# A gated delta-rule layer on one core: joint 32-block merges, weights loaded singly, index loads a job ahead, and a stated order for the first steps

## The chip, the core and the metric

The kernel runs on one core of a Trainium2 chip. Time is device time in microseconds of one execution. The engines run side by side, each through its own stream of instructions in program order: TensorE (PE, with its weight loads shown as PEld), VectorE (DVE), ScalarE (ACT), GpSimd (POOL) and SyncE (SP), which here issues every DMA. They wait for each other by semaphores.

## The reference

The input is x of 4 sequences x 512 positions x 256 channels, in float32. With xn the layer-normed x, the output is `x + s * silu(f)`, where f is a feed-forward whose weights come from a 16-entry table, and s the attention-like part:

```
qkvz = xn @ W_qkvz.T                  # 16 groups: q, k, 2 v, 2 z of 128 each
q, k, v = silu(causal conv of 4 taps, per channel)
beta = sigmoid(b);  g = -exp(A_log) * softplus(a + dt_bias)
q, k = rmsnorm(q), rmsnorm(k)         # scaled
per head: gated delta rule in chunks
    T = inverse of (I + tril(beta k k^T decay, -1))
    v_new = T v_beta - T (k_beta e^g) state
    out   = (q e^g) state + tril(q k^T decay) v_new
    state = state e^g_last + k^T v_new
s = (norm_w * rmsnorm(out) * silu(z)) @ W_out.T
f = (silu(xn @ lut[gate].T) * (xn @ lut[up].T)) @ lut[down].T
```

## The kernel before

The work is cut into 64 items: 4 sequences times 16 groups, each group with one q, one k and two value heads, over all 512 positions as four chunks of 128. An item goes through some 115 steps, each a short Python function in `STEPS`. `SLOT` (L965) is a list of step names with lags: in slot n each step `name:lag` is issued for item n - lag, so that in one slot about a dozen items are worked on, each at another stage. The order in which steps are issued is the order of every engine's stream. What is not there yet in the first slots (n - lag below 0), or no longer in the last, is simply left out.

The steps that the change touches:

- `ga` (L414) loads the 512 columns of the projection weights for q, k and both v of an item as one tile `wa`; `gz` those of z, `go` the output weights. `aq ak av0 av1` (L434) project, `y*` (ACT, L440) applies the last tap, `c*` (DVE, L446) the three others, `s*` the silu.
- `kk nt at` make the masked products, `nd nl` bring the 32 x 32 diagonal blocks to a layout of one block a partition group by DMA through DRAM, `L0` to `L3` (POOL, L621 and L627) invert them by substitution, `yd iu` bring them back by DMA into `iut`.
- `tp` (DVE, L648) turns diagonal blocks into `tpl`. `W` (L657) multiplies the off-diagonal block by one inverse, `wt` (ACT) negates and copies, `U` (L670) multiplies by the other inverse, `iu2` writes the 64-block's corner into `iut`, and `t10` turns that. `WU` (`merge2`, L687) does the same from 64 to 128: there `W2` of one item and `U2` of the item before are issued in turn, block by block, as one step.
- `ks r pv vn ps st` walk the state over the four chunks, `po sqo so ro o th h pp ac` make the output and add it to `acc`.
- `X` in the list pulls one piece of the table lookups (`lookups`, L299 on; DVE), two instructions on 344 or 256 columns. 14 jobs of 16 such pieces fill the feed-forward's weights; a job begins with the load of its indices (L316).
- `Y` lets `prepare` pull one piece of `both(b + 1)`: norm and gates of the next sequence (`normed`, `gated`). After a piece with PE work it waits three steps before the next. For sequence 1 this starts at slot 3.
- The feed-forward (`feed_forward`) fills PE where a step of the list has no item left; it starts at slot `total + 4`. Its last outputs, those of sequence 3, are kept until all else is done, since they need `acc` (L890, L891).

PSUM has eight banks, handed out in turn by `Bank`; `NBUF` says how many buffers a tile has.

Of the kernel before, what the change touches and what calls it, by code (L numbers as in the profile page):

```python
# [19 lines left out]
P = 128  # L20
# [13 lines left out]
for n, tags in {2: "v0 nt vt1 nl yl nd yd", 3: "wa qe v1 iut nk", 4: "q kd at vt0", 5: "eq", 6: "zT0 zT1", 8: "k"}.items():  # L34
    NBUF.update(dict.fromkeys(tags.split(), n))
# [3 lines left out]
def gated_delta_ffn_kernel(  # L39
# [181 lines left out]
    def gated(b):  # L221
# [3 lines left out]
        def tmp(name, shape):  # L225
            return prep.tile(shape, F32, tag=name, name=f"{name}_{b}")


        u, ab = (tmp(n, [P, 2, NC, HV]) for n in ("u", "ab"))
        graw, diff = (tmp(n, [P, NC, HV]) for n in ("graw", "diff"))  # L230
# [50 lines left out]
        gT = xs_of[b].rearrange("p c d -> p (c d)")[:HV, :S]  # L281
# [17 lines left out]
    def lookups():  # L299

        jobs = []
        for name, to, src in (("g", wg_d, gate_idx), ("u", wu_d, up_idx)):
            for d in range(DC):
                for half in range(2):
                    part = slice(half * LW, (half + 1) * LW)
                    jobs.append((f"{name}{d}{half}", to[d, :, part], src[d * P : (d + 1) * P, part]))
        for f in range(FC):
            n = min(P, INTER - f * P)
            jobs.append((f"d{f}", wd_d[f, :n, :], down_idx[f * P : f * P + n, :]))
        for name, to, src in jobs:  # L310
            n, width = src.shape
            ix, t, fx, w = (
                ffw.tile([P, LW], dt, tag=tag, name=f"{tag}_{name}")[:n, :width]
                for tag, dt in (("lt1", I32), ("lt0", F32), ("fx", F32), ("lw", F32))
            )
            moved(ix, src)  # L316
            yield

            nc.vector.tensor_copy(fx, ix)
            t1 = ffw.tile([P, LW], F32, tag="lt1", name=f"lt1f_{name}")[:n, :width]  # L320
            nc.vector.tensor_scalar(t, fx, 0.0, float(LUT), ALU.is_lt, ALU.mult)
            nc.vector.tensor_add(fx, fx, t)
            nc.vector.tensor_scalar(fx, fx, 0.0, float(LUT - 1), ALU.max, ALU.min)
            for k in range(LUT):
                if k > 1:
                    nc.vector.tensor_add(w, w, (t, t1)[(k - 1) % 2])
                nc.vector.tensor_scalar(
                    (t, t1)[k % 2] if k else w, fx, float(k), lut_b[:n, k : k + 1], ALU.is_equal, ALU.mult
                )
                yield  # L330
            nc.vector.tensor_add(w, w, (t, t1)[(LUT - 1) % 2])
            moved(to, w)
# [14 lines left out]
    SHAPES.update({"wa": [P, DC, 4 * P], "wz": [P, DC, NP * P], "wo": [P, NP, D]})  # L347
# [66 lines left out]
    @step("ga")  # L414
    def _(it):
        w = w_qkvz[:, it.hq * GW : it.hq * GW + 4 * P]
        moved(it.wa, w.rearrange("(c p) o -> p c o", p=P))
# [12 lines left out]
    def channels(x, g, block):  # L430
        def project(it):
            ps = it.put("a" + x, K)
            for d in range(DC):
                nc.tensor.matmul(  # L434
                    ps, lhsT=it.wa[:, d, g * P : (g + 1) * P], rhs=it.xnT[:, d, :],
                    start=(d == 0), stop=(d == DC - 1),
                )
# [18 lines left out]

    channels("q", 0, lambda hq: hq)
    channels("k", 1, lambda hq: HQK + hq)
    for p in range(NP):
        channels(f"v{p}", 2 + p, lambda hq, p=p: 2 * HQK + NP * hq + p)  # L460
# [191 lines left out]
    @step("W")  # L652
    def _(it):
        ps = it.put("pW")[:, : G * Q].rearrange("p (g i) -> p g i", g=G)
        for g in range(G):
            for lo, hi in HALVES:
                nc.tensor.matmul(ps[hi, g, :], lhsT=it.nt[lo, g, hi], rhs=it.tpl[lo, g, :Q], start=True, stop=True)  # L657
# [6 lines left out]

    @step("U")
    def _(it):
        ps = it.put("pU")[:, : G * Q].rearrange("p (g i) -> p g i", g=G)
        for g in range(G):
            for lo, hi in HALVES:
                nc.tensor.matmul(ps[lo, g, :], lhsT=it.wt[hi, g, :], rhs=it.iut[hi, g, hi], start=True, stop=True)  # L670
# [14 lines left out]


    def merge2(it, before):  # L687
        if before:
            pu = before.put("pU2").rearrange("p (g i) -> p g i", g=G)
        if it:  # L690
            pw = it.put("pW2").rearrange("p (g i) -> p g i", g=G)
        for g in range(G):
            if it:
                nc.tensor.matmul(pw[HI, g, :], lhsT=it.nt[LO, g, HI], rhs=it.tpl[LO, g, :], start=True, stop=True)  # L694
            if before:
                nc.tensor.matmul(
                    pu[LO, g, :], lhsT=before.w64[HI, g, :], rhs=before.iut[HI, g, HI], start=True, stop=True
                )

    @step("W2")  # L700
    def _(it):
        merge2(it, None)
# [4 lines left out]

    @step("U2")
    def _(it):
        merge2(None, it)  # L710
# [142 lines left out]
    def feed_forward():  # L853

        wgu = buffers("wa wz")[:FC]
# [19 lines left out]
        hs = buffers("ds nl")  # L875
        wd, fin, kept = [], [], []
# [6 lines left out]
        def two(ap):  # L883
            return ap.rearrange("p (j d) -> p j d", j=2)

        def finish(b, c2, y, s):
            at_ = slice(b * NC + 2 * c2, b * NC + 2 * c2 + 2)
            xr = two(in_turn("f", fin))
            moved(xr, x_t[:, at_, :])
            nc.vector.tensor_mul(y, y, s)  # L890
            nc.vector.tensor_add(y, y, xr)  # L891
            moved(out_t[:, at_, :], y)


        for b in (B - 2, B - 1, *range(B - 2)):
# [30 lines left out]
            if not wd:  # L926
                ws = buffers("v0 v1 q")
# [4 lines left out]
                held, fin = ws[3:5], ws[5:]  # L932
            for c2 in range(NC // 2):
                yield 4 * FC
                behind()
                bank = Bank(f"pd_{b}_{c2}", 1)
                for j in range(2):
                    c = 2 * c2 + j
                    for f in range(FC):
                        n = min(P, INTER - f * P)  # L940
                        nc.tensor.matmul(  # L941
                            two(bank.ap)[:, j, :], lhsT=hT[f][:n, c * P : (c + 1) * P], rhs=wd[f][:n],
                            start=(f == 0), stop=(f == FC - 1),
                        )

                def output(b=b, c2=c2, bank=bank):
                    last = b == B - 1
                    y = two(held[c2] if last else in_turn("f", fin))
                    silu(y, two(bank.read()))
                    if last:  # L950
                        kept.append((b, c2, y, acc[:, 2 * c2 : 2 * c2 + 2, :]))
                    else:
                        s = two(in_turn("f", fin))
                        moved(s, acc_d[2 * b + c2])
                        finish(b, c2, y, s)
# [3 lines left out]
        yield 1 << 30  # L959
        for late in kept:  # L960
            finish(*late)
# [4 lines left out]
        "so1:9 am:8 Y vn1:8 tk:4 cv02:3 cv11:3 ac1:11 ro1:9 cv12:3 iu:6 X o1:9 po0:8 yq:2 ps1:8 st1:8 "  # L966
        "ga:0 sqk:4 cq0:2 L0:5 pp0:11 z1:5 X sz0:5 sz1:5 tp:6 ks2:8 r2:8 go:10 po1:8 lk:4 W:6 ds:4 pv2:8 "
        "wt:6 ls:4 kk0:4 vn2:8 L1:5 ac0:11 U:6 cq1:2 eq:7 ps2:8 cq2:2 x0:4 ak:0 iu2:6 st2:8 sqo0:8 t10:6 "
        "kd:4 gz:4 ks3:8 WU:6 po2:8 x1:4 Y r3:8 pv3:8 vt1:6 kk1:4 iu4:7 vn3:8 X L2:5 yk:0 X pv0:7 po3:8 "
        "so0:8 nt0:4 nt1:4 tv0:4 vn0:7 w2:6 e:5 ro0:8 ps0:7 ck0:0 av0:2 sq:2 vt0:4 th1:9 yl:4 at0:4 tq:4 "  # L970
        "st0:7 av1:2 ck1:0 at1:4 th0:9 ck2:0 yv0:2 sqq:4 h1:9 ks1:7 cv00:2 o0:8 r1:7 cv01:2 h0:9 nd:4 "
        "nl:4 L3:5 yd:5 sk:2 sv1:4 tv1:5 pp1:10 pv1:7 aq:1 yv1:2 sqo1:8 cv10:2 g:3 z0:4 qm:5 sv0:3"
    )
    plan = [(name, int(lag or 0)) for name, _, lag in (key.partition(":") for key in SLOT.split())]
    last_lag = max(lag + (name == "WU") for name, lag in plan)
# [11 lines left out]
    items = []  # L987
# [15 lines left out]
    due = soon = 0  # L1003

    def prepare():

        nonlocal due, soon
        if soon:
            soon -= 1
            if soon:  # L1010
                return
        elif due and len(free) > 1:
            due -= 1
        else:
            return
        soon = 3 if next(preparing, None) else 0

    for n in range(total + last_lag):
        if n < total:
            items.append(Item(n))  # L1020
            b, hq = divmod(n, HQK)
            if hq == 3 and b + 1 < B:
                assert next(preparing, None) is None
                preparing = both(b + 1)
        if n == total + 4:
            for _ in looked:
                pass
            needed = next(feeding)
        for name, lag in plan:
            if name == "X":  # L1030
                next(looked, None)
            elif name == "Y":
                due += 1
            elif name == "WU":
                if item(n - lag) or item(n - lag - 1):
                    merge2(item(n - lag), item(n - lag - 1))
            elif item(n - lag):
                STEPS[name](item(n - lag))
                due += n < 2
                prepare()  # L1040
            elif needed is not None:
                spare += PASSES.get(name, 0)
                feed()
    for _ in feeding:
# [50 lines left out]
```

## Time and profile before

| what | us |
|---|---|
| median of three runs | 2115.0 (2111.66 to 2115.02) |
| the profiled execution, its own time | 2115.5 |
| its span, first to last instruction | 2113.8 |
| PE busy over the span | 2021.6 |
| DVE, ACT, POOL busy | 1771.2, 1627.2, 1370.1 |
| mean granted TensorE clock | 0.979 |

The busy time of an engine counts the stretches in which at least one of its instructions runs. A matmul of float32 is two passes in the trace (x2), each with its weight load. PE's ends are modelled, so consecutive passes overlap in the list: what a pass costs is the distance between starts. A slot is seen in the trace as the distance between the key projections of consecutive items.

### The profile page before, as it was taken

What the parts mean: (1) busy time and instruction counts of PE and PEld (TensorE: products, weight loads), DVE (VectorE), ACT (ScalarE), POOL (GpSimd) and SP (SyncE); (2) the same over time, 40 slices, a digit from 0 to 9 for tenths busy, and PEclk for the clock granted to TensorE, in tenths of its full rate; (3) what the DMA queues carried; (4) which work ended last, traced back from release to release, by engine and by line L of the source; (5) the groups of instructions that cost most, each with busy time, mean ns of one, the idle gap of its engine ahead of it and who ended that gap; (6) DMA issues with size and microseconds to landing.
All of it is one profiled execution on the core that took longest, in us unless ns stands there. A gap on an engine that the chain in (4) does not pass through costs nothing.

```text
span 2113.8 us, 48084 instructions
## 1 busy us (share of the span) xinstructions
PE 2021.6 (96%) x15744; PEld 1479.7 (70%) x15744; DVE 1771.2 (84%) x4338; ACT 1627.2 (77%) x4693; POOL 1370.1 (65%) x4181
## 2 busy tenths in 40 slices
PE   5689999999999999999999999999999999989997
PEld 3356777777776777777777777777777777776664
DVE  7878999999998999999999899999999888753322
ACT  2668888888887888888888888888888888874421
POOL 0477777777776777777767777777777777773000
PEclk8979999999999999999999999999999999998999
DMA  2333344334443434443334434344333343331202
GB/s 90 93 99 94 105 117 111 98 98 109 108 111 86 109 102 117 108 109 99 104 101 112 107 97 105 101 116 111 100 97 104 105 107 101 91 95 26 64 30 70
DMA packets 318538, 206.35 MB, mean 98 GB/s; under 512 B 221120, under 2 KB 283216, under 8 KB 318288
## 3 DMA queue, kind: packets, MB, share of 16 engines
q1 hardware_dynamic: 318288, 203.28, 36.1%
q8 instruction: 125, 2.05, 0.4%
q14 instruction: 125, 1.02, 0.2%
HBM read 179.05 MB, written 24.13 MB: 96 GB/s over the span
## 4 chain that ended last, share of the span: by engine, by line
PE 83%; DVE 6%; POOL 3%; DMA 3%; ACT 1%; issue 1%; SPq 1%; POOLq 0%; DVEq 0%; ACTq 0%
PE pp L823 10%; PE av L434 9%; PE pz L466 9%; PE pv L745 5%; PE ak L434 5%; PE po L780 5%; PE kk L544 5%; PE aq L434 4%; PE ps L758 4%; PE po L777 4%; PE ks L728 4%; PE pgu L909 3%; PE pW L694 3%; PE th L498 2%; PE ptv L498 2%; PE pd L941 2%
## 5 line engine op out<-in xcount | busy, mean ns | idle before, releaser
L621 POOL TENSOR_TENSOR pr<-nl,yl 128x60 f32<-128x60 f32 (+24 forms) x1984 | 575.1, 290 | 351.4 <-DMA nl<-nd 124.0
L627 POOL TENSOR_TENSOR yl<-yl,pr 128x60 f32<-128x60 f32 (+24 forms) x1984 | 597.7, 301 | 155.5 <-POOL pr L621 0.2
L446 DVE SCALAR_TENSOR_TENSOR v<-av,cw,v 128x509 f32<-128x509 f32 (+2 forms) x384 | 277.1, 737 | 0.8 <-ACT v L440 0.2
L434 PE MATMUL av<-xnT,wa 128*128 128x512 f32 x512 | 243.3, 598 | 1.8 <-DVE q L446 1.8
L466 PE MATMUL pz<-xnT,wz 128*128 128x512 f32 x512 | 240.9, 593 | 2.0 <-DVE vt L595 2.0
L823 PE MATMUL pp<-wo,zT 128*128 128x256 f32 x1024 | 242.4, 380 | 0.0
L823 PEld LDWEIGHTS pp<-wo,zT 128*128 128x128 f32 x1024 | 185.0, 190 | 21.7 <-issue 1.8
L86 ACT ACT_TABLE_LOAD x134 | 171.9, 1283 | 3.2 <-PEq L1085 0.8
L92 ACT ACT_TABLE_LOAD x134 | 171.9, 1283 | 1.7
L88 ACT ACTIVATE ds<-ds,ls 128x128 f32<-128x128 f32 x512 | 162.5, 391 | 10.5 <-DVE ls L520 10.4
L466 PEld LDWEIGHTS pz<-xnT,wz 128*128 128x128 f32 x512 | 96.3, 190 | 96.2 <-issue 77.0
L587 POOL TENSOR_TENSOR qe<-qe,q 128x384 f32<-128x384 f32 x128 | 125.7, 1004 | 51.2 <-DMA qe<-eg_rows 38.0
L737 DVE SCALAR_TENSOR_TENSOR r<-ks,neg,vt 128x128 f32<-128x128 f32 x384 | 116.0, 343 | 47.4 <-PE ks L728 46.9
L491 ACT ACTIVATE junk_o<-po 128x128 f32<-128x128 f32 x512 | 141.6, 277 | 13.8
L446 DVE SCALAR_TENSOR_TENSOR k<-ak,cw,k 128x509 f32<-128x509 f32 (+2 forms) x192 | 141.0, 735 | 8.5 <-ACT k L440 8.3
L446 DVE SCALAR_TENSOR_TENSOR q<-aq,cw,q 128x509 f32<-128x509 f32 (+2 forms) x192 | 141.9, 739 | 6.0 <-ACT q L440 5.9
L434 PE MATMUL ak<-xnT,wa 128*128 128x512 f32 x256 | 131.4, 639 | 13.6 <-DMA wa<-in_w_qkvz 13.6
L434 PEld LDWEIGHTS av<-xnT,wa 128*128 128x128 f32 x512 | 88.5, 192 | 66.7 <-issue 64.0
L745 PE MATMUL pv<-r,iut 128*128 128x128 f32 x768 | 124.6, 285 | 1.5 <-DVE r L737 1.5
L434 PE MATMUL aq<-xnT,wa 128*128 128x512 f32 x256 | 120.8, 594 | 0.0
L483 DVE TENSOR_SCALAR ds<-ds,gc 128x128 f32<-128x128 f32 x512 | 119.7, 303 | 0.1
L92 ACT ACTIVATE zT<-pz 128x512 f32<-128x512 f32 x128 | 75.6, 597 | 54.5 <-PE pz L466 50.6
(176 smaller groups left out, 5107.0 us busy)
## 6 DMA issues: line engine op xcount, KB each, us to landing
wa<-in_w_qkvz SPq DMA_DIRECT2D x64, 512.0 KB, 3.9
ds<-g_rows SPq DMA_DIRECT2D x64, 512.0 KB, 4.1
nl<-nd SPq DMA_DIRECT2D x256, 128.0 KB, 2.6
qe<-eg_rows SPq DMA_DIRECT2D x64, 384.0 KB, 3.6
wz<-in_w_qkvz SPq DMA_DIRECT2D x64, 256.0 KB, 2.9
wo<-in_w_out SPq DMA_DIRECT2D x64, 256.0 KB, 2.9
nd<-nt SPq DMA_DIRECT2D x256, 32.0 KB, 2.8
yd<-yl SPq DMA_DIRECT2D x256, 32.0 KB, 2.0
```

The costliest lines, as they stand in the source:

```text
L86: nc.scalar.preload_act_table_set("natural_log_exp_and_others")
L88: nc.scalar.activation(out, in_, func, **kw)
L92: nc.scalar.activation(out, in_, AF.Silu)
L434: nc.tensor.matmul(ps, lhsT=it.wa[:, d, g * P : (g + 1) * P], rhs=it.xnT[:, d, :], start=(d == 0), stop=(d == DC - 1),)
L446: nc.vector.scalar_tensor_tensor(y[:, sh:], ps[:, : S - sh], cw[:, block(it.hq), j : j + 1], y[:, sh:], ALU.mult, ALU.add)
L466: nc.tensor.matmul(ps, lhsT=it.wz[:, d, p * P : (p + 1) * P], rhs=it.xnT[:, d, :], start=(d == 0), stop=(d == DC - 1),)
L491: nc.scalar.activation(junk, ps[:, c, :], AF.Square, accum_out=out[:, c : c + 1])
L587: nc.gpsimd.tensor_tensor(it.qe[:, p], it.qe[:, p], thirds(it.q, NC)[:, 1:, :], ALU.mult)
L621: nc.gpsimd.tensor_tensor(pr[:, :k, :n], nl[:, j : j + 1, j + 1 :].to_broadcast([R * LH, k, n]), yl[:, :k, j : j + 1].to_broadcast([R * LH ...
L627: nc.gpsimd.tensor_tensor(yl[:, :k, j + 1 :], yl[:, :k, j + 1 :], pr[:, :k, :n], ALU.subtract)
L745: nc.tensor.matmul(pv[:, p, :], lhsT=it.iut[:, p * NC + c, :], rhs=it.r[:, p, :] if c else vt[:, c, :], start=True, stop=True,)
L823: nc.tensor.matmul(ps[:, j, :], lhsT=chunk(hT, 2 * c2 + j), rhs=it.wo[:, p, :], start=(p == 0), stop=(p == NP - 1),)
```

## The change

1. `W` and `U` become one step `m1`: for each of the eight blocks, W of one item (two halves) and then U of the item before it (two halves). `merge2` is the old joint 64-step, under the name `m2`.
2. `wa` is cut into `wk wq wv0 wv1` of 128 columns each, with a load step of its own for each (`gk gq gv0 gv1`).
3. `lookups` loads the indices of the next job while it works on this one, into a tile of their own.
4. `FRONT` is a list of steps with item numbers, 489 by count, issued before the slots. It covers parts of items 0 to 9: the k and q projections of eight items, v1 of seven, v0 of five, the products `nt at` of six, the substitution of four to five, W, U, W2 and U2 of items 0 to 2 (singly), the state walk of two, and the output up to `pp1` of item 0. A slot leaves out what `FRONT` has done. Gates of sequence 0 and norm and gates of sequence 1 are issued within it. `X` counts only from slot 6 on.
5. `SLOT` is another order with longer lags (up to 13, before 11), and `NBUF` other buffer counts.
6. `prepare` no longer spaces the pieces that have PE work; sequences 2 and 3 start at the middle of the sequence before.
7. The gates' temporary tiles lie in x's buffer. The feed-forward uses other buffers, starts at `total + 6`, makes outputs of one chunk at a time, fetches x and the kept sums of a sequence's four chunks ahead where buffers allow, and finishes the kept outputs before its last ones.

```diff
-for n, tags in {2: "v0 nt vt1 nl yl nd yd", 3: "wa qe v1 iut nk", 4: "q kd at vt0", 5: "eq", 6: "zT0 zT1", 8: "k"}.items():
+for n, tags in {2: "wk v0 vt0 vt1 nl yl tpl yd", 3: "v1 nt zT0 zT1", 4: "qe q iut nk", 5: "kd at", 6: "eq", 9: "k"}.items():
...
+
+        flat = xs_of[b].rearrange("p c d -> p (c d)")
+        n = NC * HV
+        u, ab = (flat[:, j : j + 2 * n].rearrange("p (a t h) -> p a t h", a=2, h=HV) for j in (0, 2 * n))
...
+        def indices(i):
+            if i < len(jobs):
+                name, _, src = jobs[i]
+                n, width = src.shape
+                ix = ffw.tile([P, LW], I32, tag="ix", name=f"ix_{name}")[:n, :width]
+                moved(ix, src)
+                return ix
+
+        ix = indices(0)
+        yield
+        for i, (name, to, src) in enumerate(jobs):
             n, width = src.shape
-            ix, t, fx, w = (
-                ffw.tile([P, LW], dt, tag=tag, name=f"{tag}_{name}")[:n, :width]
-                for tag, dt in (("lt1", I32), ("lt0", F32), ("fx", F32), ("lw", F32))
...
             nc.vector.tensor_copy(fx, ix)
-            t1 = ffw.tile([P, LW], F32, tag="lt1", name=f"lt1f_{name}")[:n, :width]
+            ix = indices(i + 1)
             nc.vector.tensor_scalar(t, fx, 0.0, float(LUT), ALU.is_lt, ALU.mult)
...
+    def weights(x, g):
+        def load(it):
+            w = w_qkvz[:, it.hq * GW + g * P : it.hq * GW + (g + 1) * P]
+            moved(getattr(it, "w" + x), w.rearrange("(c p) o -> p c o", p=P))
+
+        STEPS["g" + x] = load
...
-                    ps, lhsT=it.wa[:, d, g * P : (g + 1) * P], rhs=it.xnT[:, d, :],
+                    ps, lhsT=getattr(it, "w" + x)[:, d, :], rhs=it.xnT[:, d, :],
...
+    def merge1(it, pred):
+        pu = pred and pred.put("pU")[:, : G * Q].rearrange("p (g i) -> p g i", g=G)
+        pw = it and it.put("pW")[:, : G * Q].rearrange("p (g i) -> p g i", g=G)
         for g in range(G):
-            for lo, hi in HALVES:
-                nc.tensor.matmul(ps[hi, g, :], lhsT=it.nt[lo, g, hi], rhs=it.tpl[lo, g, :Q], start=True, stop=True)
+            if it:
+                for lo, hi in HALVES:
+                    nc.tensor.matmul(pw[hi, g, :], lhsT=it.nt[lo, g, hi], rhs=it.tpl[lo, g, :Q], start=True, stop=True)
+            if pred:
+                for lo, hi in HALVES:
+                    nc.tensor.matmul(
+                        pu[lo, g, :], lhsT=pred.wt[hi, g, :], rhs=pred.iut[hi, g, hi], start=True, stop=True
+                    )
...
-        wgu = buffers("wa wz")[:FC]
+        wgu = buffers("ds nl")[:FC]
...
-        hs = buffers("ds nl")
-        wd, fin, kept = [], [], []
...
+            def fetch(c):
+                if last:
+                    rows[c] = held[c], acc[:, c, :], xs_of[b][:, c, :]
+                else:
+                    rows[c] = [in_turn("f", fin) for _ in range(3)]
+                    moved(rows[c][1], acc_d[(b * NC + c) // 2][:, c % 2, :])
+                    moved(rows[c][2], x_t[:, b * NC + c, :])
+
+            for c in range(NC):
+                yield 2 * FC
...
+                def output(t=b * NC + c, row=rows[c], bank=bank, last=last):
+                    silu(row[0], bank.read()[:, :D])
+                    if last and slot < total + last_lag:
+                        kept.append(lambda: finish(t, *row))
                     else:
-                        s = two(in_turn("f", fin))
-                        moved(s, acc_d[2 * b + c2])
-                        finish(b, c2, y, s)
+                        finish(t, *row)
...
+        "Y qm:7 sk:5 ks1:10 z0:10 r1:10 so0:11 so1:11 h0:12 pv1:10 L0:6 cv02:7 ro0:11 vn1:10 X g:5 o0:11 "
+        "pp1:13 ro1:11 yv1:5 ps1:10 o1:11 cv10:5 iu:7 sq:5 st1:10 gv0:6 L1:6 aq:3 X yq:3 ac1:13 tk:5 "
+        "cv11:5 sqk:5 cq0:3 pp0:13 cv12:5 sz0:10 gv1:4 sv0:8 ks2:10 gq:2 r2:10 gk:0 z1:10 po0:10 sv1:6 "
+        "ac0:13 pv2:10 sz1:10 vn2:10 tp:7 po1:10 ps2:10 lk:5 m1:7 ds:5 st2:10 iu2:8 wt:7 ls:5 x0:5 ak:1 "
+        "cq1:3 gz:9 ks3:10 kk1:5 x1:5 t10:8 cq2:3 Y yk:1 r3:10 vt1:8 kk0:5 m2:8 pv3:10 kd:5 nt0:5 iu4:9 "
+        "nt1:5 L2:6 vn3:10 tq:5 X ck0:1 go:12 sqq:5 po2:10 X pv0:9 w2:8 po3:10 eq:6 nd:5 vn0:9 ck1:1 e:6 "
+        "av0:6 at0:5 ck2:1 tv0:8 yl:5 at1:5 sqo0:10 ps0:9 yv0:6 st0:9 cv00:6 th1:11 nl:5 L3:6 av1:4 "
+        "th0:11 sqo1:10 yd:6 vt0:8 tv1:7 am:9 h1:11 cv01:6"
+    )
+
+    FRONT = (
+        "yl:0 gk:0 yl:1 gk:1 gq:0 gv1:0 gv0:0 gz:0 ak:0 go:0 aq:0 yk:0 gk:2 ck0:0 ck1:0 ak:1 yq:0 gq:1 "
+        "ck2:0 cq0:0 sk:0 cq1:0 av1:0 yk:1 gk:3 cq2:0 ck0:1 sq:0 ck1:1 aq:1 yv1:0 gv1:1 ck2:1 cv10:0 sk:1 "
+        "cv11:0 kk1:0 yq:1 gq:2 cv12:0 cq0:1 tq:0 sv1:0 tk:0 cq1:1 sqq:0 ak:2 cq2:1 sqk:0 eq:0 aq:2 gk:4 "
+        "yk:2 g:0 sq:1 ck0:2 e:0 kk0:0 ck1:2 e:1 yq:2 ck2:2 gq:3 kk1:1 e:2 cq0:2 sk:2 e:3 cq1:2 av1:1 cq2:2 "
...
+        "sv1:6 so0:1 ks3:1 sqq:6 tv0:3 r3:1 U2:2 nl:5 vt0:3 pv3:1 vt1:3 pp1:0 ds:6 iu4:2 vn3:1 gv1:7 tp:3 "
+        "av0:4 ro0:1 L2:4 ac1:0"
...
+            while next(preparing, None):
+                pass
+
+    for name, _, m in (key.partition(":") for key in FRONT.split()):
+        m = int(m)
+        while len(items) <= m:
+            items.append(Item(len(items)))
+        if (name, m) == ("g", 0):
+            for _ in preparing:
+                pass
+            preparing = both(1)
+        done.add((name, m))
+        STEPS[name](items[m])
+        due += 8 < len(done) < 40 or len(done) % 8 == 0
+        prepare()
     for n in range(total + last_lag):
         if n < total:
...
-        if n == total + 4:
+        if n == total + 6:
...
-                next(looked, None)
+                if n >= 6:
+                    next(looked, None)
...
+            elif name in MERGES:
+                it, pred = (
+                    None if (half, m) in done else item(m) for half, m in zip(HALF[name], (n - lag, n - lag - 1))
+                )
+                if it or pred:
+                    MERGES[name](it, pred)
...
+    slot = total + last_lag
+    for late in kept:
+        late()
```

## The prediction

> **What bounds the kernel now.** I read the busy times of the page first, then busy times by stage, then the order of time inside one slot, then the end.
>
> ```profile
> PE 2021.6 (96%) x15744; PEld 1479.7 (70%) x15744; DVE 1771.2 (84%) x4338; ACT 1627.2 (77%) x4693; POOL 1370.1 (65%) x4181
> PEclk8979999999999999999999999999999999998999
> ```
>
> PE is busy for 96% of the span, but that is an average over a front, a steady part and a drain. The stages tell more (length, then busy time of PE, PEld, DVE, ACT, POOL, then the granted clock):
>
> ```profile
> 0.00:200.00 200.00, 145.14 (x832) 89.14 (x833) 157.16 (x377) 114.48 (x303) 99.27 (x311) 0.87 0.34 97
> 757.90:1015.60 257.70, 257.70 (x2144) 193.07 (x2144) 245.62 (x607) 222.37 (x651) 193.74 (x587) 1.00 0.41 107
> 1452.90:1681.80 228.90, 228.90 (x1905) 171.47 (x1904) 210.29 (x523) 197.17 (x577) 170.03 (x522) 1.00 0.40 106
> 1681.80:1767.90 86.10, 86.10 (x719) 64.56 (x718) 72.11 (x176) 74.21 (x218) 62.39 (x196) 1.00 0.38 102
> 1800.00:2100.00 300.00, 284.60 (x1718) 201.33 (x1717) 127.78 (x300) 144.95 (x394) 92.50 (x285) 0.96 0.22 61
> 2100.00:2113.80 13.80, 0.00 (x1) 0.00 (x0) 3.97 (x6) 0.60 (x1) 0.00 (x0) 0.64 0.39 121
> ```
>
> The second to fourth rows hold 9, 8 and 3 slots, cut where consecutive items' key projections start: 28.63, 28.61 and 28.70 us a slot, with PE never idle. There, PE work is time. DVE takes 245.62 / 9 = 27.3 us of a slot while 344-wide lookups run, 26.3 with 256-wide ones and 24.0 without any; ACT 24.7. The first 200 us lose 55 us to idle PE and 0.13 x 200 = 26 us to the clock, 81 in all. The drain loses 15 + 12 = 27 us, the end 13.8.
>
> **Joint merges.** One slot's merges, in order of time (start, length):
>
> ```profile
> 1012.16 0.39 PE L780 MATMUL po<-vnB,at 128*128 128x128 f32 x2
> 1012.48 0.69 PE L657 MATMUL pW<-tpl,nt 32*32 32x32 f32 x32
> 1013.10 0.71 PE L745 MATMUL pv<-r,iut 128*128 128x128 f32 x4
> 1013.65 0.39 PE L544 MATMUL kk<-k 128*128 128x128 f32 x2
> ...
> 1014.65 0.69 PE L670 MATMUL pU<-iut,wt 32*32 32x32 f32 x32
> 1015.27 0.71 PE L758 MATMUL ps<-vnA,kd 128*128 128x128 f32 x4
> ...
> 1018.17 0.22 PE L694 MATMUL pW<-tpl,nt 64*64 64x64 f32 x1
> 1018.18 0.22 PE L696 MATMUL pU<-iut,w 64*64 64x64 f32 x1
> 1018.23 0.22 PE L694 MATMUL pW<-tpl,nt 64*64 64x64 f32 x1
> ```
>
> Two full passes start 0.22 us apart, so W should start at 1012.38: 0.10 lost going in, 0.62 until the next group, which then takes 0.55 us to its successor where four full passes take 0.44: 0.11 lost coming out. W costs 0.83 us, U the same, 1.66 a slot. Inside W a pass lasts 0.19, so 32 starts lie in 0.50 us, 16 ns apart, or 32 ns for a pair on its two corners of the array. The 64-wide merge, already joint, starts W and U some 7 ns apart and repeats a corner after 58 ns. 58 for 64 columns and 32 for 32 look like the time one corner needs for its own next weights. W and U together use four different corners, and four starts of 7 ns fit in 32. Then the joint merge takes W's 0.83 and saves 0.83 a slot. If instead 16 ns is what any small pass costs, 64 take 1.02 + 0.12 + 0.21 = 1.35 and 0.31 is saved. I take the first, since the 7 ns row contradicts a plain limit of 16, and keep both ends; a loss is excluded, since the passes are the same and one way in and out (0.21) is dropped.
>
> The Trainium skill (TensorE: Matmul & The Clock Gate, section "Wait — 56ns, not 53.3ns?") states that starts never come closer than about 25 ns however small the matmul. By it the 64 passes take 1.6 us, and the merge would cost about what W and U cost now: nothing gained. The trace has 16 and 7 ns, so it disagrees, and I go by the trace.
>
> Worth: of the 60 joint merges (the list does the first three items singly) I count 22 slots with DVE at 27.3 of the new 27.8 us; there DVE is at 98% and I grant half, 0.41 x 22 = 9 us. Some 25 later slots have DVE at 26.3 or less: 0.83 x 25 = 20.5. The last 13 fall into the drain, where PE is not always the limit: half, 5.5. **Sum 35**, bounds 13 (0.31 in 47 slots, less in the drain) and 50 (0.83 x 60).
>
> **The front.** Counting the 489 names of the list and multiplying by durations of rows (a projection 1.72 on PE; a tap 0.72 on DVE, of which it has 81; four squares 1.73 on ACT; a quarter solve 4.85 on POOL) I get PE 104.5, DVE 121, ACT 118 with its 14 table loads, POOL 98 us. The same per-step prices give 26.15 us of DVE for a whole item, and the fourth row has 24.0, so I scale DVE by 0.92 to 111. Norm and gates add some 10 us each to PE and DVE, and to ACT 6 plus up to eight more table loads of 1.28, 16 in all. Steps start about 12 us in. DVE is through at 133 at best, ACT at 146, with 114 us of PE work done: 32 us lost. Slots 0 to 8 are then empty but for lookups, slots 9 and 10 nearly; their 20 lookups put 17 us on DVE beside 4 on PE, and slots 11 and 12 are DVE's too, so the best loss is about 38. The same sum for the old order, through slot 15: 349 x 0.92 + 17 + 12 = 350 against 310 of PE work, 40 lost at best, and 81 were. So 41 us came from latency: PE waited 18 us for the first tpl and 13.6 for wa. The list has many independent projections ahead of the first W, so I grant it half, 20 us, on top of 38: loss 58, **gain 23**. Bounds 2 (all 41 us of latency stay) and 43.
>
> **What I cost at nothing.** *Weights singly*: three more issues an item at 0.45 us; SP issues take about 10 us of a slot, 11.7 after; the first weights come as 128 KB, not 512. The stages hide it; without that cover 1.35 a slot. *Index loads ahead*: DVE waited 11 us in total for indices, under a busy PE; at DVE's 98% up to 5 might count. *One more iut and tpl to zero*: 1.6 us of DVE before the first statistics, hidden because ACT waits for a_log until 8.1 us anyway. *Norm and gates in one go*: ACT then waits behind six PE groups a sequence, about 1 us each, 18 in all at three sequences; ACT's 3 us of slack a slot hides it. *Single 64-wide merges of three items*: about 3 us, in an unfilled front. *u, ab, graw, diff in x's buffer*: written after the transposes have read it, as the data demand anyway. *Narrower feed-forward outputs, a drain two slots longer in lags with feeding two slots later*: -20 to +20 us around the 27 lost now; nearest row is that loss itself, so 0.
>
> **The end.**
>
> ```profile
> 2097.92 2.08 PE L941 MATMUL pd<-ff_v,ff_nl 128*128 128x256 f32 x8
> 2105.87 0.69 DVE L891 TENSOR_TENSOR ff_v<-ff_v,ff_q 128x512 f32<-128x512 f32 x1 [2.77 <-DMA ff_q<-in_x]
> 2109.87 0.69 DVE L891 TENSOR_TENSOR ff_v<-ff_v,ff_q 128x512 f32<-128x512 f32 x1 [2.71 <-DMA ff_q<-in_x]
> ```
>
> After the last matmul at 2100.0 two kept outputs run one after the other, each waiting 2.7 us for its x. The change runs them before and loads x ahead, so one 256-wide output stays: 0.45 + 0.41 + 0.41, 2.1 for the output to land, 1.1 to the end, about 5. **Gain 9**, bounds 0 and 10.
>
> **Sum.** The profiled execution took 2115.5 us (span 2113.8 and 1.7 around it), 0.5 over the median of 2115.0. 2115.5 - 35 - 23 - 9 = 2048.5; I say **2049**.
>
> **Rivals.** *Issue limit*: four corners don't overlap, 16 ns a pass. For it: W and U alone show 16. Against: 7 ns in the 64-wide merge. 2115.5 - 13 - 23 - 9 = 2070. *DVE takes over*: at 27.3 us plus the 1.3 it idles in a slot now (it waits for ks and ps) the slot stays at 28.6 in the 22 lookup slots, and the front keeps its latency: 2115.5 - 26 - 2 - 9 = 2078. *The list doesn't fill the front and the end grows in the drain*: 2115.5 - 35 - 2 + 10 = 2088. *Slower: ACT becomes the bound.* The new slot puts readers right behind PE steps: no PE work lies between aq and yq (2.6 us before), pv1 and vn1 (3.4), W and wt (0.4). ACT, in order, then waits where it didn't. It works 24.7 and idles 3.9 us a slot; three new waits of 0.6 make 30.4, 1.8 over the old slot, hence 1.8 x 47 = 85 more: 2115.5 + 85 - 23 - 9 = 2168. It decides once ACT idles over 4.6 us a slot, where the slot's 0.7 x 47 us eat the 32 of front and end. Against: today's idle is largely waiting that PE's pace sets, and PE's lead is not read from a list.
>
> **Chances.** Forecast 0.47 (its own range 2020 to 2066), issue limit 0.17, DVE 0.16, no front 0.10, ACT 0.10. A measurement of this kernel can tell about 0.2% (4 us) from no change. Slower 0.10; within 0.2%, between the last two cases, 0.03; faster 0.87. All best ends give 2115.5 - 50 - 43 - 10 = 2012; leaving out ACT's case, the range ends 10 us past the fourth case: 2010 to 2098.
>
> **What would show it.** Slots of 27.8 us with PE never idle; one block of 64 small passes about 0.6 us long; in the first 200 us a loss of PE near 58, with DVE and ACT both near 0.85 busy until about 160; under 6 us after the last matmul. Wrong: a block of 1.1 us or more; slots at 28.6 with DVE or ACT over 97%; a front that still waits for tpl.

## The result and the profile after

The changed kernel takes 2081.8 us (median of 4 runs, 2079.3 to 2082.5), the kernel before 2115.0: a ratio of 0.9844 (0.9826 to 0.9861), or 33 us less. Forecast were 66 us less. The profiled execution of after took 2079.3 us, its span is 2077.1.

The first view is the page of after: busy time, share of the span and instructions of an engine, then the granted clock in 40 slices.

```profile
PE 1982.1 (95%) x15744; PEld 1450.0 (70%) x15744; DVE 1779.2 (86%) x4356; ACT 1624.0 (78%) x4691; POOL 1385.6 (67%) x4181
PEclk9988899999999999999999999999999999999999
```

PE does the same 15744 passes in 39.5 us less busy time (2021.6 before), and the share of PE is a point lower: more of what is left is idle. The stages of after (length, then busy time of PE, PEld, DVE, ACT, POOL, then the granted clock):

```profile
0.00:200.00 200.00, 147.02 (x860) 92.88 (x860) 153.04 (x358) 126.52 (x339) 115.11 (x362) 0.91 0.36 95
784.70:1038.00 253.30, 252.27 (x2146) 189.33 (x2142) 243.22 (x601) 223.65 (x649) 197.40 (x587) 1.00 0.42 110
1441.90:1666.20 224.30, 223.83 (x1913) 168.54 (x1905) 213.10 (x536) 198.81 (x577) 172.26 (x521) 1.00 0.42 108
1666.20:1721.90 55.70, 55.70 (x480) 42.10 (x476) 48.57 (x117) 49.67 (x145) 41.97 (x132) 1.00 0.38 103
1777.10:2077.10 300.00, 285.55 (x1744) 198.40 (x1744) 134.57 (x310) 133.14 (x387) 75.58 (x230) 0.98 0.23 64
2073.10:2077.10 4.00, 0.00 (x0) 0.00 (x0) 0.85 (x2) 0.38 (x1) 0.00 (x0) 1.00 0.10 33
```

Rows two to four hold 9, 8 and 2 slots, of 28.14, 28.04 and 27.85 us (28.63, 28.61 and 28.70 before). DVE is busy for 96% of the second row and PE still for 99.6%. The fifth row takes the last 300 us of the span, with the 4.0 us of the sixth in it. After the last pass these 4.0 us are left; before it was 13.8.

To see where the 36.7 us of span went I price every PE pass at its steady duration in the kernel before (a 32-wide one 26 ns, a 512-wide one 430 ns, and so on), add up the passes begun by a moment, and take the sum from the time. This "loss" holds idle PE and the halved clock, and it falls where passes get cheaper. Its growth by stage, worked out from the traces, us:

```
                                  before   after   gain
to 250 us                          83.8    102.4   -18.6
250 us to 300 us before last pass  14.3    -14.6    28.9
the last 300 us of passes          34.8     18.2    16.6
after the last pass                13.8      4.1     9.7
```

The front got worse, the steady part and the end came out near the forecast, and the drain, forecast at about 5, gave 17. Single losses hang on the prices and are good to some 3 us; the gains hardly depend on them.

This is the place in the front, windows of after in the columns of the stages above:

```profile
180.00:190.00 10.00, 7.50 (x48) 3.16 (x46) 9.53 (x22) 2.93 (x7) 8.28 (x24) 1.00 0.07 19
190.00:200.00 10.00, 1.04 (x4) 0.71 (x4) 9.76 (x20) 0.69 (x1) 8.51 (x22) 0.50 0.00 0
200.00:210.00 10.00, 0.04 (x1) 0.00 (x0) 9.47 (x20) 2.07 (x11) 8.20 (x24) 0.50 0.46 106
210.00:220.00 10.00, 8.44 (x101) 6.02 (x102) 5.64 (x14) 5.54 (x16) 5.96 (x21) 0.64 0.03 8
```

PE has nothing for 22 us while DVE is full. What PE waited for between 180 and 240 us (total, times, longest), and what DVE did meanwhile (start, length):

```profile
PE pW L672 <- DVE tpl L660: 11.5, 2, 11.0
PE ptk L510 <- DVE k L456: 11.5, 1, 11.5
```

```profile
193.37 0.52 DVE L333 TENSOR_TENSOR lw_g<-lw_g,lt_g 128x344 f32<-128x344 f32 x1
193.81 0.39 DVE L334 TENSOR_SCALAR lt_g<-fx_g,lut_b 128x344 f32<-128x344 f32 x1
194.23 0.52 DVE L333 TENSOR_TENSOR lw_g<-lw_g,lt_g 128x344 f32<-128x344 f32 x1
194.67 0.39 DVE L334 TENSOR_SCALAR lt_g<-fx_g,lut_b 128x344 f32<-128x344 f32 x1
195.09 0.52 DVE L333 TENSOR_TENSOR lw_g<-lw_g,lt_g 128x344 f32<-128x344 f32 x1
195.53 0.44 DVE L334 TENSOR_SCALAR lt_g<-fx_g,lut_b 128x344 f32<-128x344 f32 x1
195.89 0.73 DVE L456 SCALAR_TENSOR_TENSOR k<-ak,cw,k 128x509 f32<-128x509 f32 x1
```

The list of 489 steps is through at about 181 us. The slots behind it are nearly empty, since their steps are done, but each still issues its four pieces of the lookups. So in DVE's stream 15 pieces (slots 6 to 9; the first only issues a load) stand in a row, from 181.6 to 195.9 us, ahead of the first tap (L456) of the item that PE needs next. Seven more stand among the taps that follow, ahead of the tpl that ends PE's second wait (DVE turns it at 210.4).

### The profile page after: what moved, and what is told of

Its sections match the earlier page's. It is cut to its first block, busy times and chain, and to the rows that moved or that the text cites. A ratio compares the mean times of both kernels' runs of the same rounds, so it can differ in the third digit from the quotient of the medians.

```text
span 2077.1 us, 48707 instructions
## 1 busy us (share of the span) xinstructions
PE 1982.1 (95%) x15744; PEld 1450.0 (70%) x15744; DVE 1779.2 (86%) x4356; ACT 1624.0 (78%) x4691; POOL 1385.6 (67%) x4181
## 4 chain that ended last, share of the span: by engine, by line
PE 72%; DVE 20%; ACT 4%; DMA 2%; issue 1%; SPq 1%; POOL 0%; DVEq 0%; ACTq 0%; POOLq 0%
PE av L444 8%; PE pp L824 8%; PE pz L478 7%; PE pv L746 5%; PE po L781 4%; PE aq L444 4%; PE ak L444 4%; PE pgu L907 4%; PE kk L556 4%; PE po L778 3%; PE ps L759 3%; PE ks L729 3%; DVE v L456 3%; PE pW L703 2%; PE th L510 2%; PE pd L956 2%
## 5 line engine op out<-in xcount | busy, mean ns | idle before, releaser
L633 POOL TENSOR_TENSOR pr<-nl,yl 128x60 f32<-128x60 f32 (+24 forms) x1984 | 585.3, 295 | 173.9 <-DMA nl<-nd 11.4
L456 DVE SCALAR_TENSOR_TENSOR v<-av,cw,v 128x509 f32<-128x509 f32 (+2 forms) x384 | 282.5, 736 | 7.6 <-ACT v L450 6.7
L444 PE MATMUL av<-xnT,wv 128*128 128x512 f32 x512 | 245.4, 602 | 5.5 <-ACT ds L88 3.6
L88 ACT ACTIVATE ds<-ds,ls 128x128 f32<-128x128 f32 x512 | 156.9, 389 | 1.5
L503 ACT ACTIVATE junk_o<-po 128x128 f32<-128x128 f32 x512 | 142.2, 278 | 15.2 <-PE po L781 2.9
L456 DVE SCALAR_TENSOR_TENSOR q<-aq,cw,q 128x509 f32<-128x509 f32 (+2 forms) x192 | 142.3, 741 | 7.5 <-ACT q L450 5.3
L456 DVE SCALAR_TENSOR_TENSOR k<-ak,cw,k 128x509 f32<-128x509 f32 (+2 forms) x192 | 141.5, 737 | 3.5 <-ACT k L450 2.9
L444 PEld LDWEIGHTS av<-xnT,wv 128*128 128x128 f32 x512 | 88.5, 193 | 70.4 <-issue 63.0
L444 PE MATMUL ak<-xnT,wk 128*128 128x512 f32 x256 | 130.8, 635 | 4.4 <-ACT junk_q L503 4.4
L746 PEld LDWEIGHTS pv<-r,iut 128*128 128x128 f32 x768 | 105.4, 191 | 39.7 <-issue 29.7
L444 PE MATMUL aq<-xnT,wq 128*128 128x512 f32 x256 | 124.0, 607 | 3.6 <-DMA wq<-in_w_qkvz 2.5
```

The source lines that it names most:

```text
L88: nc.scalar.activation(out, in_, func, **kw)
L444: nc.tensor.matmul(ps, lhsT=getattr(it, "w" + x)[:, d, :], rhs=it.xnT[:, d, :], start=(d == 0), stop=(d == DC - 1),)
L456: nc.vector.scalar_tensor_tensor(y[:, sh:], ps[:, : S - sh], cw[:, block(it.hq), j : j + 1], y[:, sh:], ALU.mult, ALU.add)
L503: nc.scalar.activation(junk, ps[:, c, :], AF.Square, accum_out=out[:, c : c + 1])
L633: nc.gpsimd.tensor_tensor(pr[:, :k, :n], nl[:, j : j + 1, j + 1 :].to_broadcast([R * LH, k, n]), yl[:, :k, j : j + 1].to_broadcast([R * LH ...
L746: nc.tensor.matmul(pv[:, p, :], lhsT=it.iut[:, p * NC + c, :], rhs=it.r[:, p, :] if c else vt[:, c, :], start=True, stop=True,)
```

## The experiments

Each ratio below is to the kernel before in the same round of runs, where it took 2108 to 2112 us (2115 in the round of the change). So differences between medians of different rounds are good to some 5 us, and the spans and losses of the profiles stand beside them where they matter.

### The front

Six runs. The first moves the lookups behind the empty slots:

```
             if name == "X":
-                if n >= 6:
+                if n >= 11:
                     next(looked, None)
```

> The lookup pieces count only from slot 11 on instead of 6; all of them are still done, and end some five slots later. Theory (lookups in empty slots): the 16 to 20 pieces of slots 6 to 10 stand on DVE ahead of the taps and of tp, at a time when PE has nothing else; the two waits of PE of 11.5 and 11.0 us and most of the half clock after them go, so the kernel takes 2047 to 2060 us and the loss of PE at 300 us falls from 103 to 70 to 80. Rival (the list ends on the latency of the inversion chain, DMA and POOL, whatever DVE does): the waits stay, 2075 to 2082. Rival (DVE takes the pieces back later): the first waits go, but the slots after 11 are longer by as much, 2070 to 2080.

Measured: 2063.8 us, ratio 0.9781 (0.9752 to 0.981), 18 us faster than the change by medians, 20 by spans and 13 by the ratios; once more on another chip 2065.3, 0.9792 (0.9774 to 0.9811). A loss of 85 at 250 us instead of 102. Its windows in the place of the hole:

```profile
190.00:200.00 10.00, 3.86 (x67) 2.39 (x68) 8.91 (x20) 3.98 (x16) 7.96 (x27) 0.70 0.37 91
200.00:210.00 10.00, 9.57 (x56) 6.22 (x54) 6.97 (x18) 5.66 (x19) 7.89 (x27) 0.96 0.31 58
```

PE works 13.4 us in the 20 us in which it had worked 1.1. The loss of 85 is nevertheless above the 70 to 80 that the theory gave, and the time above its 2047 to 2060; of the rivals, neither came. The opposite edit, `n >= 3`, puts 12 more pieces there; and `n >= 13` asks for the best place:

> The kernel after the change with lookups from slot 3, which puts 12 more pieces of 0.87 us into the same hole behind the list. Theory (DVE's lookups hold PE there one for one): 8 to 11 us more than the 2081.8 after the change, 2088 to 2094. Rival (PE waits there for something else): within 3 us of it.

> Lookups count from slot 13 on. Theory (every piece ahead of slot 13 stands on DVE where DVE, not PE, is the limit): the 8 pieces of slots 11 and 12, some 7 us, are worth 3 to 7: 2055 to 2061. Rival (from slot 11 on PE or POOL is the limit): within 2 us of x11, 2062 to 2066.

Measured: 2087.4 (0.9887, 0.9859 to 0.9915), 6 us more than the change by medians and 10 by spans, with a loss of 113 at 250 us; and 2064.3 (0.9774, 0.976 to 0.9789), the same as slot 11. The first lies just under the 8 to 11 us of its theory by medians and inside by spans: pieces in the hole cost about their own DVE time. The second came out as its rival said: slot 11 is late enough.

Is the list itself worth anything? The next run leaves it empty, with the lookups from slot 0 and the second sequence's norm and gates begun at slot 3:

```
-    FRONT = ( ... )
+    FRONT = ""
...
-            if b and hq == HQK // 2 and b + 1 < B:
+            if n == 3 or b and hq == HQK // 2 and b + 1 < B:
...
-                if n >= 6:
+                if n >= 0:
...
+                due += n < 2
```

> The list of first steps is empty; the slots issue everything, lookups from slot 0, norm and gates of sequence 1 from slot 3 as before. Theory (the list was worth a little until 180 us, and lost it all to the lookups behind it): the front loses what it lost before the change, 84 us, and up to 10 more for two slots of longer lag, against 103 now; 2062 to 2075 us. Rival (the list does fill the front, and the longer lags cost much without it): 2090 us or more.

Measured: 2080.2 us, ratio 0.9866 (0.9832 to 0.9899), level with the change and between theory and rival. Its loss at 250 us is 106, where the kernel before, filled by slots too and with the lookups from slot 0 too, has 84. PE's longest waits of this run in the first 300 us:

```profile
PE pW L672 <- DVE tpl L660: 39.8, 7, 21.4
PE tpx L213 <- DVE xs L204: 12.4, 2, 11.5
PE av L444 <- DMA wv<-in_w_qkvz: 10.2, 2, 9.4
```

In the kernel before the same wait took half as long in that window:

```profile
PE pW L657 <- DVE tpl L648: 18.8, 7, 11.9
```

So without the list the rest of the change fills the first 250 us worse than the kernel before, by 22 us. The first W comes no later (103 us, 107 before), but PE runs out of other work ahead of it: it idles 21.4 us there, while DVE is nearly idle too (busy for 1.4 us between 90 and 100). That points at the longer lags, with the weights that come singly (wv) for some of it; neither was tried alone.

What the list is worth by itself is not shown. With it the loss is 102, 4 less than without, and 85, 21 less, once the lookups are out of its way. But the 21 hold two things: the lookups take 48.7 us of DVE in the first 250 us without the list, 27.3 in the change and 10.6 with slot 11 (38.5 before). The slots alone with the lookups from slot 11, and the kernel before with the same shift, were not run.

What paces the list? POOL's substitution is busy for some 15.8 of every 20 us from 100 us on. One run leaves out every second of its 31 steps for items 0 to 4, so that it no longer works out the whole inverse; another takes the second sequence's norm and gates out of the list and issues them in slots 10 to 20:

```
-        for j in range(8 * part, min(8 * part + 8, Q - 1)):
+        for j in range(8 * part, min(8 * part + 8, Q - 1), 2 if it.n < 5 else 1):
```

> Lookups from slot 11, and the substitution of items 0 to 4 leaves out every second of its 31 steps. Theory (POOL paces the list: its first block lands at 69 us, and 4.75 solves of 22.7 us each, two instructions a step, end at 177 to 182, where PE leaves the list): POOL saves some 50 us, the list ends 20 to 40 us earlier, where ACT and DVE take over; the loss of PE at 300 us falls from 85 to 45 to 65, and the kernel takes 2025 to 2045 us. Rival (hand-overs between PE, ACT and DVE pace the list): the loss stays at 80 to 85, 2057 to 2066.

> Lookups from slot 11; norm and gates of sequence 1 are issued in slots 10 to 20 instead of in the list. Theory (POOL paces the list, so these 10 us of DVE and 16 of ACT are hidden there): nothing gained in the list, and DVE, near its limit behind it, takes them on: 2062 to 2075. Rival (ACT or DVE pace the list): 5 to 12 us less, 2050 to 2058.

Measured: 2059.6 (0.9754, 0.9734 to 0.9773) and 2061.7 (0.9759, 0.9742 to 0.9776), 4 and 2 us under slot 11 alone. Half the substitution moves the loss at 180 us from 71.5 only to 67.2, and 4 us at the end, as its rival said; POOL is not what paces the list. Norm and gates, with a result just under the theory's 2062, are no cost worth naming where they are. What keeps PE from its work between 20 and 180 us is spread over many waits of 1 to 5 us on DVE, ACT and DMA, with the clock between 0.74 and 1.00; no single one was found.

### The joint merge

All W passes first, then all U passes, in one block:

```
         for g in range(G):
             if it:
                 for lo, hi in HALVES:
                     nc.tensor.matmul(pw[hi, g, :], ...)
+        for g in range(G):
             if pred:
```

> The joint step issues all 16 multiplications of W, then all 16 of U, at the same place. Theory (each corner of the array is held about 32 ns by its own reload, four corners run at once): the block is 0.5 us longer, 0.5 x 60 = 30 us at most where PE is the limit; 2100 to 2112 us, slots of 28.4. Rival (the gain came from one way in and out less, or from the new places of the steps): under 5 us more, slots stay at 27.9.

Measured: 2093.4 us, ratio 0.9925 (0.9898 to 0.9951), 12 us more than the change by medians and 16 by spans, less than the theory's 18 to 30 and more than the rival's 5. The shortest slots, those in which PE waits for nothing, are 28.2 us long where after has 27.9. The trace says why: the 64 starts of a block lie in 0.92 us instead of 0.56. Then W and U apart, with full passes between them, as before the change:

```
-        "... vn2:10 tp:7 po1:10 ps2:10 lk:5 m1:7 ds:5 ..."
+        "... U:8 vn2:10 tp:7 po1:10 ps2:10 lk:5 W:7 ds:5 ..."
```

> Lookups from slot 11, and the 32-wide merge apart again: U of item n-8 alone before vn2, W of item n-7 alone where the joint block stood, full passes between them. Theory: two ways in and out and no overlap cost 0.75 us a slot in the 50 steady slots, some more in the drain: 35 to 50 us more, 2098 to 2115. Rival: what the joint block gains lies under DVE at 97 percent in the slots with lookups, now nearly all, so that only 5 to 20 us are lost: 2068 to 2085.

Measured: 2097.0 us, ratio 0.9945 (0.9931 to 0.996): 32 us over the same kernel with the joint block. In the steady part the loss grows by 18.7 where slot 11 alone has it fall by 15.2, 34 us apart; in the drain the two differ by 1. The time is just under the theory's range. The shortest slots are 28.6 us, as in the kernel before. So one block instead of two is worth some 0.4 us a slot, and the alternation in it another 0.35. The passes of the two kernels, first apart and then a joint block of after, which lasts from 1009.47 to 1010.03 (start, length):

```profile
1037.92 0.69 PE L675 MATMUL pU<-iut,wt 32*32 32x32 f32 x32
1038.54 0.49 PE L778 MATMUL po<-stA,qe 128*128 128x128 f32 x2
...
1040.08 0.69 PE L672 MATMUL pW<-tpl,nt 32*32 32x32 f32 x32
1040.70 1.98 PE L444 MATMUL ak<-xnT,wk 128*128 128x512 f32 x4
```

```profile
1009.47 0.22 PE L672 MATMUL pW<-tpl,nt 32*32 32x32 f32 x2
1009.48 0.22 PE L675 MATMUL pU<-iut,wt 32*32 32x32 f32 x2
1009.52 0.20 PE L672 MATMUL pW<-tpl,nt 32*32 32x32 f32 x2
1009.54 0.20 PE L675 MATMUL pU<-iut,wt 32*32 32x32 f32 x2
1009.55 0.20 PE L672 MATMUL pW<-tpl,nt 32*32 32x32 f32 x2
1009.57 0.20 PE L675 MATMUL pU<-iut,wt 32*32 32x32 f32 x2
```

A round of four corners begins every 32 ns (1009.52, .55, .59), so U rides in W's time. With DVE at 96% the joint block still pays in nearly every slot: the rival, in which its gain lies under DVE, had forecast a loss of only 5 to 20 us.

### The index loads

Here each load is issued in its own job again, first with nothing between the load and its first reader, then with the pause of one piece that the kernel before had (`yield` behind the load):

```
+            if i:
+                ix = indices(i)
             nc.vector.tensor_copy(fx, ix)
-            ix = indices(i + 1)
```

> Lookups from slot 11, and each index load is issued at the start of its own job again, not one job ahead. Theory: a load takes about 3 us and is hidden under the other work of a slot in which PE is the limit; the 16 jobs cost together 0 to 5 us, as the prediction had it. Rival: DVE is at 97 percent in the slots with lookups, so that every wait of 2 to 3 us shows in full: 16 times 2.5 us, 30 to 40 us more.

> Lookups from slot 11, and each index load in its own job with the pause of one piece between load and first read, as the kernel before had it. Theory: the pause, a quarter of a slot, hides most of the load, so that the 43 us of the run without a pause shrink to 0 to 5 us over the kernel with loads a job ahead: 2063 to 2070. Rival: the pause does not help, as the load waits in the queue of transfers for longer than a piece lasts: 2085 to 2108.

The yardstick of these two and of the runs on the drain is the repeated run:

> The changed kernel with the pieces of the lookups starting in slot 11 once more, as the yardstick for the three runs beside it. Theory: 2059 to 2067 us, as before.

Measured: 2106.6 us (0.9994, 0.9981 to 1.0007) without a pause and 2074.9 (0.9837, 0.9823 to 0.9852) with it, beside 2065.3. So 41 and 10 us; the theory gave at most 5 for both, and missed both. Without a pause the rival came, with it neither. The waits of DVE, then of PE, in the run without a pause from 300 to 1750 us (total, times, longest):

```profile
DVE fx_d L328 <- DMA ix_d<-in_down_idx: 15.5, 6, 2.8
...
DVE fx_u L328 <- DMA ix_u<-in_up_idx: 12.1, 4, 3.4
DVE fx_g L328 <- DMA ix_g<-in_gate_idx: 9.9, 3, 3.7
```

```profile
PE pz L479 <- DVE acc L837: 36.3, 13, 4.4
PE pW L704 <- DVE r L739: 2.0, 4, 0.8
```

Thirteen loads, 37.5 us of waiting on DVE, and 36.3 us on PE, 2.9 and 2.8 each: the sum into acc (L837) stands behind the copy in DVE's stream, and PE needs the bank that it frees. With the pause DVE waits for five loads only, 8 us, and PE 10.2 us in other places:

```profile
PE th L512 <- DVE at L566: 10.2, 4, 3.8
```

### Drain and end

Four runs: the kept outputs finished after the feed-forward instead of before its last passes (on the change itself); the feed-forward from slot 72 (`total + 8`) instead of 70; the outputs' rows of x never loaded a sequence ahead (the lines with `more` gone); the outputs in pairs, 512 wide, as before (all three with lookups from slot 11).

```
-    for late in kept:
-        late()
     for _ in feeding:
         pass
+    for late in kept:
+        late()
```

> The four kept outputs of sequence 3 are finished after the feed-forward's last output, as before the change, but with x loaded ahead. Theory (what was saved at the end is above all the wait for x): four times a product and a sum of 0.43 us each and their stores behind each other, 2 to 5 us more. Rival (it is the order that saved the 10 us): 8 to 10 us more.

> Lookups from slot 11, and the feed-forward starts at slot 72 instead of 70. Theory: the drain lost 27 us before and about 10 less after because its holes get feed-forward passes early enough; with two slots less of filler the holes of slots 70 and 71 stay open, and the time grows by 5 to 15 us over the same kernel with slot 70. Rival: the filler is only moved, as much of it is left over at the end either way, and what shortened the drain are the lags: within 4 us.

> Lookups from slot 11, and the outputs of the feed-forward never get the buffers that k leaves, so their rows of x are loaded one output ahead and not a sequence ahead. Theory: PE paces the drain, the outputs have their rows in time, within 4 us. Rival: outputs wait for their rows as they did after the last matmul before (2.7 us each), and the drain grows by 10 us or more.

> Lookups from slot 11, and the outputs of the feed-forward in pairs, 512 wide on one bank and one pause of the plan for two, as before. Theory: the narrow outputs fill the holes of the drain in finer steps; with pairs the drain loses 5 to 12 us more, 2069 to 2076, and the end after the last matmul grows by 0.4 to 1. Rival: the lags and the order of steps made the drain shorter, and the width is worth under 3 us: 2061 to 2068.

Measured: 2082.2 (0.9866, 0.9837 to 0.9895), 2060.6 (0.9775, 0.9754 to 0.9796), 2066.4 (0.9804, 0.9782 to 0.9825) and 2063.1 (0.9781, 0.9765 to 0.9798). Finishing the kept outputs last lengthens the end from 4.1 to 7.2 us in the profiles (3.1 in the span), as the theory had it; the medians can't tell it. The other three stay within some 5 us of their yardstick: the later feed-forward and the pairs came out as their rivals said, the rows of x as the theory said. In all of them the last 300 us lose 16 to 19 us, in the other runs with the new slot 16 to 21, and 34.8 in the kernel before. Of the 16.6 us between before and after, PE's idle time makes up 4 (15.5 us of the last 300 before, 11.3 after) and the clock some 7 (a mean of 0.960 before, 0.983 after). What is common to all these runs and not to the kernel before is the order and the lags of the new slot, with its buffer counts and the singly loaded weights. A run with the old order alone and the rest new was not made, so that this is where it points, and not shown.

## Why the prediction missed by half

*Joint merges, 35 forecast: right in mechanism.* The shortest slots fall from 28.64 to 27.87 us where 27.8 was named, a block lasts 0.56 us where 0.6 was, and there is no limit of 16 ns a pass. The floor of about 25 ns between starts that the Trainium skill states (TensorE: Matmul & The Clock Gate, section "Wait — 56ns, not 53.3ns?") would, by an estimate of 64 such starts, have made the block 1.6 us long; the trace disagrees, with 0.56. Undoing the joint block whole costs 32 us. That slots with lookups would give only half was wrong in its reason: the block pays there too, and something else in the new slot takes part of it back. In the 49 slots 11 to 59 the fall of 0.77 us would be 38; but what the slots take beyond the shortest one grew from 21.5 us in all to 32.6, and 27 are left. With the block apart it is 26.0, so that some 6 of the block's 38 come back as waiting. Nor do the effects seen one by one add up: 34 for the block and about 11 for the loads, against 29 that the steady part gained. So the remaining edits of the slot cost about 16 there by this sum, if the effects add; no run shows which. That the steady part met its forecast is therefore luck in part.

*The front, a gain of 23 forecast: wrong, and the step that failed.* It forecast a loss of 58; there were 102, 18.6 more than before. Two things were mis-stated. First, "their 20 lookups put 17 us on DVE beside 4 on PE" was added to DVE's total, as work that could go on beside others. It is a place in a stream in order: 15 pieces in a row, with the next item's taps behind them, stop PE for 11.5 us, seven more among the taps hold up tpl for 11 more, and the clock is halved for 27 us. That is 13 to 20 us, by taking them away (17 of the loss). Second, the sum took 20 us of latency off the old kernel's 41 and put the lags of the new slot at nothing in the front. With the lookups out of the way the loss is still 85, 27 above the forecast, and without the list the rest of the change loses 22 more than the kernel before. The trace points at the lags, but which part of the change it is stays open. That the list ran to 181 us and not 160 I had not foreseen either: none of my totals of work was above 146. The waits in the list are many and short; what makes it take 181 us was not found.

*Index loads, forecast 0, "at DVE's 98% up to 5 might count":* 10 to 13 us, by medians and by spans, in the new order of steps. The wait of 11 us in the profile before looked hidden under a busy PE; what it cost in the old order was not tried. Whether a wait is hidden depends on what stands behind it on its engine.

*The drain, forecast 0 beyond 5.5 from the merges:* 17 us, inside the stated bounds of 20, with a cause left open, and not from the merges. *The end, forecast 9:* 9.7, with 4.0 us after the last pass; about 3 of it come from finishing the kept outputs early. *Norm and gates in one go, forecast 0:* right within 2 us, as far as it was tried (the second sequence). *Weights singly:* PE's waits for weights fell from 13.6 us in the front (wa) to 2.5 (wq); the part was not tried apart. The rival of a bound on ACT didn't come: ACT has 24.8 us of a 28.1 us slot.

So 23 - (-18.6) = 42 us were missed in the front; 11 more in the drain, and small sums elsewhere, gave a part back. The best versions that were run all have the lookups from slot 11 and take 2061 to 2066 us; the differences among them are too small to rank.

## What to carry to other kernels

Where a part of an order is issued ahead, look at what remains in the slots that it empties: filler that stood between other steps stands there in one row, and an in-order engine puts it in front of the work that everyone waits for. Price a wait on an engine by what is queued behind it and who needs that, not by its length, since 2.9 us of a load on DVE became 2.8 us on PE each time. Before longer lags are paid for by a list, price the lags by themselves in the fill.

## What the runs showed of the hardware

Four 32-wide passes on four corners started 6 or 7 ns apart, a round every 32 ns, as long as W and U alternate; 64 starts lay in 0.56 us. Later in the same block the pairs drifted apart, to gaps of 1 and 15 ns, with the same 32 ns a round. With all W ahead of all U the 64 starts took 0.92 us, and 0.50 for each half alone, so that the halves overlapped for less than 0.1: U's first passes started among W's last.

After PE fell idle at 187.5 us the granted clock went to a half at 189.9 and stayed there for 27.3 us, some 6 us beyond the end of the second wait at 211, so that the hole of 22 us cost more than its length, by some 3 us (an estimate: half of these 6).
